# Expert products in the batches of blocks 0 to 2: a half-cost floor on the planner's PE budget

## The chip, the cores and the metric

The kernel runs on one core of one Trainium2 chip. The metric is device time in microseconds (us), the median over executions: 1169.55 us before the change (three runs, 1169.44 to 1170.32). The profile is of one further execution. Its engines are called PE (the matrix engine), DVE (vector), ACT (scalar), POOL and SP, as in the profile.

## The reference, cut to what matters

Two transformer layers over x, four sequences of 512 tokens, 256 wide, all in float32. The change touches the plan of layer 0 only.

```python
x = x + attn0(layernorm(x))      # 16 heads of 16, causal, softmax
x = x + experts(layernorm(x))    # below
x = x + attn1(layernorm(x))      # 16 heads of 128, 4 kv heads; mixes the 4 sequences at one position
x = x + mlp(layernorm(x))        # gelu(gate) * up, 2048 wide, 4-bit weights

# experts: 8 of them, one choice of two for every token AND output column
logits = (h @ router_w.T + router_b).reshape(T, 256, 8)
w, sel = top_k(softmax(logits), 2);  w = w / w.sum()
c      = zeros(T, 8).at[t, sel].add(w)          # summed over the 256 columns
final  = einsum('te,teo->to', c, h @ expert_w.T + expert_b)
```

For each group of 128 tokens the experts need two sets of 256x2048 products, one for the router's logits and one for the experts' outputs, and between them a long elementwise search for the two greatest of eight logits.

## The kernel before, in words

**Layer 0's attention** runs in 44 batches. Block j holds 512 rows: a quarter of the positions of all four sequences. A batch is one block, one sequence s and some of the four groups of four heads: all four groups in block 0 (batches 0 to 3), two in block 1 (4 to 11), one in blocks 2 and 3 (12 to 27 and 28 to 43). The loop at L833 does the following for batch n, and every engine but SP runs its instructions in exactly this order:

- `greatest(n+1)`, L652: PE computes the scores of the next batch, into four of the five PSUM tiles of `ps_sc` (L454).
- `shift(n)`: PE transposes the maxima (`mxT`, L681), DVE subtracts them from the queries (`qk`, L684).
- `mask(n+1)`: PE adds the causal mask (L665), DVE takes the maxima, four reductions (L671), which lets those PSUM tiles go.
- **slot a**: a call of `fill` (L849).
- `mixed(n-1)`, L736: PE multiplies the previous batch's probabilities with the values.
- `powers(n)`: PE computes the shifted scores (L700) into four tiles of `ps_sc`, ACT takes exp of each (L709), which lets them go.
- **slot b**: a call of `fill` (L857).

**fill** is a planner that works while the program is written out: it fixes the order, and nothing of it runs on the chip. It gives PE and DVE a budget in about microseconds (PE 2.0 and 2.4 in slots a and b of blocks 0 and 1, 1.8 and 2.2 in block 2, 1.6 and 2.0 in block 3; DVE 2.6 in each). What was overdrawn in the slot before is taken off; what was left over is lost. It then goes through the streams in their order, and takes a stream's next piece as long as that engine's budget is above zero and the piece's own condition holds. A piece may overdraw.

The streams that matter here, in the order in which they are asked:

- `divided` (L748): the end of a sequence's attention: `av_T`, `oq_T`, and after a block's last sequence two output products of cost 1.75 (L783).
- `hidden_pieces` (L264): the second layernorm of a finished block and its transposes.
- `addition_pieces` (L341): DVE adds the experts' weighted outputs (L350 to L352), cost 1.55 for half a group.
- `total_pieces` and `weight_pieces` (L432, L355): DVE's search over one group's logits, 17 steps in all. It starts with L371 and L373, cost 1.25 each, and ends with eight steps of 0.95 (L423, L426). Group g's search starts only in a slot after the one that wrote its last logit product. `weights[g]` is set when a group is done.
- `result_pieces` (L302): the expert products `eo`, cost 1.85, four to a group; ACT scales and evicts each (L323).
- `logit_pieces` (L282): the logit products `lg_ps`, cost 1.85, four to a group; ACT copies each out (L297).

Both kinds of product wait on `made()`, the number of the search's steps planned so far divided by 17. With the group under search counted as k, its steps release products in this order: eo 0 of group k-1 at step 0, lg 0 of group k+1 at 2, then eo 1 at 4, lg 1 at 6, eo 2 at 8, lg 2 at 10, eo 3 at 12 and lg 3 at 13. All products are `dense` (L228): two fp32 matmuls, which the profile shows as four rows of 128x512.

What is not done at the end of layer 0's attention is worked off in layer 1's attention. There `between` (L1124) gives a `fill` after nearly every piece, with a PE budget of `1.9 * share + 0.2`; `share` (L1141) is the number of products still open over the slots up to step 8, and is zero from step 9. At step 10 a loop (L1128) plans whatever is then left.

Of the kernel before, what the change touches and what calls it, by code (L numbers as in the profile page):

```python
# [32 lines left out]
def tile_transformer(  # L33
# [75 lines left out]

    slot = 0

    def need(engine, cost, gap=0, cond=None):
        return engine, cost, gap, cond
# [1 line left out]
    class Stream:  # L117
# [4 lines left out]
        def ready(self, left):  # L122
            if self.next is None:
                return False
            engine, cost, gap, cond = self.next
            return left[engine] > 0 and slot >= self.last + gap and (cond is None or cond())

        def go(self):
            engine, cost = self.next[:2]
# [17 lines left out]
    left = {"PE": 0.0, "DVE": 0.0}  # L147
# [113 lines left out]
    logits, weights, halves = {}, {}, {}  # L261
# [187 lines left out]
    with ExitStack() as l0:  # L449
# [377 lines left out]
        done = blanked = 0  # L827
# [479 lines left out]
```

## Time and profile before

| What | Value |
|---|---|
| Median of three runs | 1169.55 us |
| Profiled execution, its own time | 1170.3 us |
| Its span on the core | 1168.6 us |
| Granted PE clock, mean | 1.00 |
| Logit products, L234 `lg_ps` | 122.5 us busy, 256 rows |
| Expert products, L234 `eo` | 121.5 us busy, 256 rows |
| DVE's maxima, L671 | 100.4 us busy, 176 rows |
| PE idle while DVE waits: `qk` L684 for `mxT` | 29.0 us in 14 waits |

The span covers all but 1.7 us of the profiled execution. The busy time of PE counts rows whose ends are modelled and which overlap, and a matmul that is held up by a wait shows as a long row; so PE's 98% does not say that it never waits. Time stamps below are us from the start of the span. Layer 0's attention runs from about 26 to 376 us, layer 1's attention from about 394 to 834, and the mlp to the end. Batches 12 to 27, block 2, lie between about 127 and 250 us.

### The profile page before, as it was taken

How to read it: one execution, taken by the hardware profiler on the slowest of the kernel's cores; microseconds unless marked ns; L12 is line 12 of the kernel's file. 1: busy time of each engine (PE TensorE's matmuls, PEld its weight loads, DVE VectorE, ACT ScalarE, POOL GpSimd, SP SyncE). 2: the span in 40 equal slices, each digit the busy share in tenths (PEclk: the TensorE clock that was granted, in tenths of full speed). 3: DMA queues.
4: the chain of work that ended last, by engine and by line, in shares of the span. 5: the costliest groups of instructions: out<-in, count | busy, mean ns of one | idle time of the engine just before them, and what ended most of it. 6: DMA issues, size and time to landing. Idle time of an engine off the chain costs nothing.

```text
span 1168.6 us, 18563 instructions
## 1 busy us (share of the span) xinstructions
PE 1142.0 (98%) x7178; PEld 661.5 (57%) x7178; DVE 809.8 (69%) x1783; ACT 484.3 (41%) x1099; POOL 108.4 (9%) x152
## 2 busy tenths in 40 slices
PE   7999999999999999999999999999999999999998
PEld 3666555556554445555555555566644475484487
DVE  5676889999988953868773785687699845716710
ACT  1444645556555542444443444544344312303300
POOL 7322221212112000000000000000000000000000
PEclk9999999999999999999999999999999999999999
DMA  7230110000000500000000001120110000000000
GB/s 219 64 83 2 19 20 2 2 1 2 2 2 1 181 1 1 1 1 1 1 1 1 1 1 46 28 54 21 27 46 1 0 1 19 0 1 19 1 18 19
DMA packets 21239, 26.46 MB, mean 23 GB/s; under 512 B 5128, under 2 KB 14600, under 8 KB 21152
## 3 DMA queue, kind: packets, MB, share of 16 engines
q1 hardware_dynamic: 20480, 24.10, 7.5%
q10 hardware_dynamic: 672, 1.18, 0.4%
q8 instruction: 56, 0.92, 0.3%
q14 instruction: 31, 0.25, 0.1%
HBM read 18.97 MB, written 2.10 MB: 18 GB/s over the span
## 4 chain that ended last, share of the span: by engine, by line
PE 81%; DVE 13%; ACT 2%; issue 1%; POOL 1%; DMA 0%; SPq 0%; ACTq 0%; DVEq 0%; POOLq 0%
PE qk_ps L987 11%; PE y L1234 9%; PE o L1078 9%; PE g L916 9%; PE u L916 9%; PE lg_ps L234 8%; PE eo L234 7%; PE s L652 3%; PE s L700 3%; DVE mx L671 3%; PE av L736 2%; PE v_ps L969 2%; PE qk_ps L545 2%; PE a L1058 1%; PE s L1000 1%
## 5 line engine op out<-in xcount | busy, mean ns | idle before, releaser
L987 PE MATMUL qk_ps<-xT,wqkv 128*128 128x512 f32 x320 | 148.9, 599 | 2.3 <-ACT part L323 1.2
L234 PE MATMUL lg_ps<-rw,xT 128*128 128x512 f32 x256 | 122.5, 601 | 1.4 <-ACT xT L954 0.3
L234 PE MATMUL eo<-ew,xT 128*128 128x512 f32 x256 | 121.5, 600 | 0.8 <-ACT lg L297 0.5
L1078 PE MATMUL o<-wpj,oT 128*128 128x256 f32 x512 | 119.1, 382 | 0.0
L1234 PE MATMUL y<-wd,it 128*128 128x256 f32 x512 | 111.8, 379 | 0.0
L1078 PEld LDWEIGHTS o<-wpj,oT 128*128 128x128 f32 x512 | 95.9, 190 | 27.5 <-issue 14.3
L1234 PEld LDWEIGHTS y<-wd,it 128*128 128x128 f32 x512 | 97.0, 190 | 15.0 <-issue 2.2
L671 DVE TENSOR_REDUCE mx<-s 128x1 f32<-128x384 f32 (+3 forms) x176 | 100.4, 632 | 1.3 <-PE s L665 1.3
L987 PEld LDWEIGHTS qk_ps<-xT,wqkv 128*128 128x128 f32 x320 | 59.1, 190 | 71.4 <-issue 57.4
L709 ACT ACTIVATE pt<-s 128x512 f32<-128x512 f32 (+1 forms) x176 | 84.1, 563 | 35.3 <-PE s L700 35.3
L916 PE MATMUL g<-xT,wgu 128*128 128x512 f32 x192 | 90.4, 593 | 0.0
L916 PE MATMUL u<-xT,wgu 128*128 128x512 f32 x192 | 90.2, 592 | 0.0
L323 ACT ACTIVATE part<-eo,c 128x256 f32<-128x256 f32 x128 | 53.7, 472 | 85.2 <-PE eo L234 75.2
L719 POOL TENSOR_SCALAR_AFFINE_SELECT pt<-pt 128x256 f32<-128x256 f32 (+2 forms) x88 | 63.2, 725 | 249.8 <-ACT pt L709 249.3
L1212 ACT ACTIVATE th<-sq 128x512 f32<-128x512 f32 x64 | 40.3, 630 | 87.6 <-DVE sq L1211 87.6
L234 PEld LDWEIGHTS lg_ps<-rw,xT 128*128 128x128 f32 x256 | 46.1, 190 | 46.1 <-issue 37.3
L234 PEld LDWEIGHTS eo<-ew,xT 128*128 128x128 f32 x256 | 46.1, 190 | 45.7 <-issue 38.3
L222 DVE TENSOR_TENSOR xres<-xres,y 128x256 f32<-128x256 f32 x16 | 6.7, 421 | 92.5 <-PE y L1234 92.5
L185 POOL TENSOR_TENSOR ln_rs<-rs_v,minus_half 128x4 f32<-128x4 f32 x16 | 17.6, 1099 | 552.2 <-DVE rs_v L184 439.9
L297 ACT COPY lg<-lg_ps 128x512 f32<-128x512 f32 x64 | 37.6, 588 | 73.5 <-PE lg_ps L234 73.5
L1213 DVE SCALAR_TENSOR_TENSOR th<-th,g 128x512 f32<-128x512 f32 x63 | 43.2, 686 | 29.2 <-ACT th L1212 29.2
L916 PEld LDWEIGHTS u<-xT,wgu 128*128 128x128 f32 x192 | 36.5, 190 | 45.9 <-issue 44.7
(233 smaller groups left out, 1776.8 us busy)
## 6 DMA issues: line engine op xcount, KB each, us to landing
qk<-stage SPq DMA_DIRECT2D x56, 64.0 KB, 2.4
wqkv<-in_w_qkv SPq DMA_DIRECT2D x8, 320.0 KB, 6.8
rw<-in_router_w SPq DMA_DIRECT2D x8, 256.0 KB, 7.8
ew<-in_expert_w SPq DMA_DIRECT2D x8, 256.0 KB, 4.6
wpj<-in_w_proj SPq DMA_DIRECT2D x1, 2048.0 KB
out<-xres SPq DMA_DIRECT2D x4, 512.0 KB, 2.6
xres<-in_x SPq DMA_DIRECT2D x3, 512.0 KB, 9.0
dq_wgu<-in_gate_w SPq DMA_DIRECT2D x8, 128.0 KB, 2.4
```

The source lines that it names most:

```text
L234: nc.tensor.matmul(ps, lhsT=xT[:, hc, (g % 4) * P : (g % 4 + 1) * P], rhs=w[:, hc, 2 * pair : 2 * pair + 2, :].rearrange("p e o -> p (e o) ...
L297: nc.scalar.copy(lg[:, 2 * pair : 2 * pair + 2, :].rearrange("p e o -> p (e o)"), ps)
L323: nc.scalar.mul(part[:, e % 4], ps[:, i], c[:, e : e + 1])
L671: nc.vector.tensor_reduce(maxes[n % 2][:, h, gs[0] : gs[0] + nb], ps[:, : nb * nk].rearrange("p (b k) -> p b k", b=nb), AX.X, ALU.max,)
L709: nc.scalar.activation(pt[:, i, : nb * nk], tiles[2 * pair + i][:, : nb * nk], AF.Exp, scale=0.25)
L719: nc.gpsimd.affine_select(out=last, in_=last, compare_op=ALU.is_ge, fill=0.0, base=0, pattern=pattern, channel_multiplier=-1,)
L916: nc.tensor.matmul(ps, lhsT=wgu[:, w, half, jj, par * P : (par + 1) * P], rhs=xT[:, half, :], start=half == 0, stop=half == 1,)
L987: nc.tensor.matmul(ps, lhsT=wqkv[:, hc, kv, h, :], rhs=xT[:, hc, :], start=hc == 0, stop=hc == 1,)
L1078: nc.tensor.matmul(ys[t // 2][:, t % 2], lhsT=state["o"][:, h, t * P : (t + 1) * P], rhs=wpj[:, HPK * kv + h, :], start=kv == 0 and h == 0 ...
L1212: nc.scalar.activation(th, sq, AF.Tanh, scale=0.7978845608028654)
L1213: nc.vector.scalar_tensor_tensor(th, th, 1.0, gp, ALU.add, ALU.mult)
L1234: nc.tensor.matmul(ps, lhsT=it[:, c // 2, c % 2, t * P : (t + 1) * P], rhs=wd[:, c // 2, c % 2, :], start=c == 0, stop=c == 2 * NJ - 1,)
```

## The change: a product is planned only while half its cost is left

```diff
-    slot = 0
+    slot = done = 0
...
             engine, cost, gap, cond = self.next
-            return left[engine] > 0 and slot >= self.last + gap and (cond is None or cond())
+
+            least = cost / 2 if engine == "PE" and cost > 1.8 and weights and done < 28 else 0.0
+            return left[engine] > least and slot >= self.last + gap and (cond is None or cond())
```

Only the two kinds of product have a PE cost above 1.8. For them the budget must now exceed 0.925 and not just zero. `weights` is empty until the search over group 0 is done, so the rule begins there. `done` counts the batches whose powers are planned; it is 28 after `powers(27)`, so the last slot under the rule is slot a of batch 27. The loop's own `done = blanked = 0` (L827) now sets the name that line 112 has introduced. No instruction is added, removed or changed in kind.

## The prediction

> **What bounds the kernel.** I read the page first (engines, chain), then the busy time by stages, then the chain of waits and the timelines of PE and DVE between 150 and 255 us, the only stretch in which the rule acts, and last the waits of the later stages. The stages (PE, PEld, DVE, ACT, POOL busy, then the granted clock):
>
> ```profile
> 154.00:250.00 96.00, 94.59 (x949) 50.83 (x945) 89.19 (x219) 55.33 (x157) 20.92 (x27) 1.00 0.01 1
> 440.00:706.00 266.00, 264.02 (x1258) 148.34 (x1257) 177.56 (x440) 115.36 (x302) 1.01 (x1) 1.00 0.00 1
> ```
>
> In layer 1 (second row) PE is full and DVE has a third of its time free. Work that the change pushes from layer 0 into layer 1 therefore costs there what it saves before. In block 2 (first row) PE and DVE are both above 92%, and hand over to each other in every batch: `shift` on DVE needs `mxT` from PE, `powers` on PE needs `shift` and the reductions. What one engine loses by the other's late handover is the only thing that a new order can win. The chain from batch 22 to 24 shows such a loss:
>
> ```profile
> 211.95 1.91 PE eo L234 x4
> 213.86 1.72 PE lg_ps L234 x4
> 215.58 0.86 PE s L652 x8
> 216.44 0.26 PE mxT L681
> 216.70 0.22 PE s L665 x4
> 216.92 1.77 PE lg_ps L234 x4
> 218.69 0.79 PE av L736 x24
> 219.49 0.88 PE s L700 x24
> 220.37 2.29 PE s L652 x6
> 222.66 0.26 PE mxT L681
> ```
>
> Slot b of batch 22 holds a pair, eo and lg; slot a of 23 one lg; slot b of 23 nothing, for the powers (L700) are followed at once by the next scores (L652). These take 2.29 us where the same work took 0.86 five lines above: the trace shows their weights waiting for ACT's exps, which must empty the PSUM tiles. While the pair ran, DVE had used its share and stood:
>
> ```profile
> 216.74 0.29 DVE L684 TENSOR_TENSOR qk<-qk,mxT 128x128 f32<-128x128 f32 x1 [2.09 <-PE mxT L681]
> 246.05 0.29 DVE L684 TENSOR_TENSOR qk<-qk,mxT 128x128 f32<-128x128 f32 x1 [1.62 <-PE mxT L681]
> ```
>
> The second line is the same pattern one group later (pair in slot b of batch 26, nothing in slot b of 27, where the scores take 2.68 against 1.14 us). A third, weaker pair stands in slot b of batch 17: DVE waits 1.05 us at 180.79, and both slots of batch 19 are empty (`powers` 1.42 against 0.95, scores about 2.5 against 0.93).
>
> **The change part by part.** *What it forbids.* After one product of 1.85 at most 2.4 - 1.85 = 0.55 is left, under 0.925, so no slot under the rule takes two. After an output product (1.75) at most 0.65 is left: none there either. A debt of more than about 0.9 also shuts a slot of 1.8, but with one product per slot debts stay near 0.2. From 154 to 248 us, 25 slots hold 23 products. The demand fits one to a slot; three pairs must be split, and one product that now stands beside an output product's debt (lg at 151.5, slot a of 14) is put off.
>
> *Its price on PE.* In the chain a product behind another takes 1.72 us, behind the mask 1.77, behind the powers 1.91. Some six products change place: at most 6 x 0.19 = 1.1 us, mostly 0.05 each; I take 0.3, and it is inside the steps below. [...] The row has clock 1.00 throughout 154 to 250 us, though the stalls are in it; the gaps now get shorter. I take the row: nothing.
>
> *First product, 151 us.* Put off to slot a of 16, which pushes the next lg to the empty slot b there. From 151 to 173 us DVE is busy without a break (L684 at 159.63 stands behind five search steps), so the earlier end on PE is worth nothing, and the later extra 1.9 us lies where PE waits for DVE anyway (`oq`, `xn` at 172). Nothing either way; without that cover it would be 1.9 us moved.
>
> *Pair of batch 17.* Without the second product the scores of batch 18 end about 1.5 us earlier, and DVE's `shift` 1.04 us earlier: it ends its own work at 179.75. The three products behind it move one place; the last fills slot a of 19. Followed forward, batch 20's powers, held up by 0.41 us (`av`) and 0.58 us (`powers` 1.53 against 0.95), come **1.4 us** earlier.
>
> *Pair of batch 22.* DVE goes from 214.65 straight into `shift`: about 2 us more for it. PE has lg 2 in slot a of 23 and lg 3 in slot b; that fills the hole before the scores. The 1.43 us of stall (2.29 - 0.86) goes, less 0.3 for the product's later start: PE is **1.1 us** further ahead, 2.5 in all. What is late next: lg 3 now comes in slot b of 23, so the next search cannot start there. L371 and L373 (2.5 of budget) slip one slot and DVE's gain goes into idle time.
>
> *Pair of batch 26.* By the step counts, eo 2 (step 8) is not yet released in slot a of 26, because the search is late and step 8 must wait one slot more. It goes to slot b, eo 3 to slot a of 27, and lg 2 and lg 3 come together in slot b of 27, where the rule has ended. A hole (26a) and a pair (27b) remain, in place of a pair (26b) and a hole (27b); the shift of 27 still comes without DVE's wait of 1.62 us, about half of which reaches PE: **0.8 us**. Sum 1.4 + 1.1 + 0.8 = 3.3 us at 250 us, with as many products done as before, but the search one slot behind (two steps of 0.95 and L371: 3.15 of budget).
>
> *Block 3, given back.* In slot a of 28 lg 0 now lacks its step and slips to slot b. The empty slot costs about what the reductions outlast the mask and `av`: 2.48 (L671) + 0.3 - 0.8 - 0.9 = 1.1 us at most, nothing if the product fills a later hole (slot b of 36, where the scores take 2.12 against 1.14). I take 0.6. Block 3's small budgets then keep its slots at one product each, one product behind; that one ends up in layer 1 at cost. No DMA, POOL or SP instruction moves past another one; `sum_up` on ACT keeps its place relative to its steps.
>
> Sum: 3.3 - 0.6 = **2.7 us less**: 1170.3 - 2.7 = 1167.6 for the profiled execution, and with the 0.75 us by which that lies above the median, 1166.8 us.
>
> **The rivals.** *Moved, not removed* (1168.5; within 0.2%, which is 2.3 us and about what a measurement of this kernel can tell). For it: half of what I count at each pair is DVE time that DVE then idles away, and in block 3 both engines are again above 92% with a pipeline in a worse phase, so 28a, 30 and 41 may each cost 0.5 to 1 us. Against: the scores' long rows are PE's own loss, and PE's time decides the end.
>
> *Holes elsewhere, too* (1163.5): a smoother train also closes holes in block 3 (DVE waits 2.51 at 328.93 and 1.65 at 361.24, `o0` waits 1.74 for `aT` at 382.12). Against: the rule is off there.
>
> *The search starves* (1174). Every group's lg 3 comes at step 13 and lies at the end of a row of four products released within six steps. At one to a slot it is a slot late, and DVE loses up to 2.6 of budget for each group. If this does not stop after two groups but carries through block 3, where slots have less PE budget, four to six groups lose a slot each and PE gets holes of about 1.1 us each: 4 to 6 us, or 1174. It decides if by the end of layer 0 two or more further products are open. In layer 1 the last search step of group 15 is at 691.3 us and step 8's last slot at about 703; if the search is over 12 us late there, the last products fall where `share` is zero and wait for one another, some 3 us more. For it: period and slots agree to the digit (8 slots and 8 products to a group), so no slot is spare for a late one. Against: DVE waits 5.01 and 2.33 us in layer 1's tail, so there the search is waited for by nobody but itself.
>
> *The rule hardly acts*: it decides only where the budget lies between 0 and 0.925; 3 pairs and one single product here. That is in the sums.
>
> **How the numbers follow.** Forecast 0.45 (1165.0 to 1168.2), holes elsewhere 0.07, moved but not removed 0.25, starved 0.23. Forecast and holes give faster 0.52. For 8 in 10: from 1163.0, below the hole case, to 1172.0, within the starved one; 4 to 6 us above is cut off.
>
> **What would show it.** Right: no two products side by side between 154 and 248 us; no scores row above 2 us at about 220; DVE's waits of 2.09 and 1.62 us gone; the first 32x512 scores (244.61 before) some 3 to 5 us earlier; the first layer-1 product (394.51) about 4 us earlier, with one product less before it. Wrong: if that mark comes earlier only by the 1.72 us of each product left out, nothing was won; if L371 of groups 3 to 7 comes later than at 221.34, 252.29, 294.45 and 331.81, the search is starved[...].

## The result, and the profile after

| Kernel | Median | Runs |
|---|---|---|
| before | 1170.26 us | 6 |
| after | 1175.39 us (1173.14 to 1176.82) | 6 |

The ratio is 1.0046, with a 95% interval of [1.0036, 1.0056]: the change makes the kernel slower by 5.1 us, where 2.7 us less was forecast, and the time lies above the range (1163.0 to 1172.0). The profiled execution of after is its fastest run, 1173.14 us, with a span of 1171.4. In the code after the change every line behind the edit stands two further down: L236 is the products, L673 the maxima, L686 `qk`.

First the busy time by stages, after; columns as before (length, then PE, PEld, DVE, ACT, POOL busy, the granted clock, the DMA's share and GB/s).

```profile
154.00:250.00 96.00, 93.47 (x956) 49.38 (x960) 90.68 (x225) 57.28 (x162) 18.56 (x29) 1.00 0.01 1
250.00:376.00 126.00, 121.06 (x1385) 68.51 (x1374) 110.76 (x262) 71.16 (x183) 22.30 (x34) 1.00 0.01 2
```

The same stretch of block 3, before, which the prediction did not print:

```profile
250.00:376.00 126.00, 123.10 (x1405) 68.59 (x1404) 116.10 (x264) 73.30 (x192) 22.29 (x35) 1.00 0.01 2
```

In block 2, where the rule acts, DVE now does more in 96 us (90.68 against 89.19). In block 3, where the rule is off, DVE does 5.3 us less and PE 2.0 us less. That is the first sign that the loss is not where the edit is.

**Block 2 gives the sum that was forecast.** The chain of waits of after, at the batches that the prediction showed (start, length, engine, tile, line, rows):

```profile
209.68 1.91 PE eo L236 x4
211.59 0.86 PE s L654 x8
...
212.93 1.77 PE lg_ps L236 x4
...
216.38 1.91 PE lg_ps L236 x4
218.29 0.86 PE s L654 x8
```

The pair is gone: one product in slot b of 22, one in slot a and one in slot b of 23, and the scores that took 2.29 us take 0.86. DVE's waits of 2.09 and 1.62 us, which were to go, have not gone; each stands one batch later. From DVE's timeline (start, length, and in brackets the idle time before it):

```profile
219.45 0.29 DVE L686 TENSOR_TENSOR qk<-qk,mxT 128x128 f32<-128x128 f32 x1 [2.01 <-PE mxT L683]
249.18 0.29 DVE L686 TENSOR_TENSOR qk<-qk,mxT 128x128 f32<-128x128 f32 x1 [1.79 <-PE mxT L683]
```

Added up over 154 to 250 us, DVE waits 3.8 us for `mxT`, against 5.3 before.

**Marks, compared.** Every batch has one `mxT`, and by it the two traces can be laid side by side. Differences to before in us, with the shift of the whole trace at batch 0 taken off; "open" is how many products fewer had been done by then, and the last column adds 1.75 us for each of them (the length of a product behind another or behind the mask):

| Mark | Before | After | open | at equal work |
|---|---|---|---|---|
| `mxT` of batch 20 | 192.20 | -0.4 | 0 | -0.4 |
| batch 22 | 207.95 | -2.2 | 0 | -2.2 |
| batch 24 | 222.59 | -3.4 | 0 | -3.4 |
| batch 28 | 252.12 | -3.2 | 0 | -3.2 |
| batch 29 | 260.01 | -4.9 | 2 | -1.4 |
| batch 37 | 321.04 | -5.1 | 2 | -1.6 |
| batch 40 | 343.35 | -3.1 | 3 | +2.1 |
| batch 43 | 366.29 | -3.2 | 2 | +0.3 |
| first layer-1 product | 394.51 | -2.7 | 3 | +2.5 |
| scores of step 1 of layer 1 | 446.24 | -0.6 | 4 | +4.6 |
| scores of step 9 | 690.11 | +2.9 | 0 | +2.9 |

(Step 1 has one `v_ps` product more done, which is taken off.) Up to batch 28 the change wins 3.2 us, almost to the digit what was forecast. Then it loses in four places (and wins 1.8 us back between batches 40 and 43).

*Batch 28* loses 1.8 us. DVE's timeline of after, the end of one search and the start of the next:

```profile
252.45 0.42 DVE L425 SCALAR_TENSOR_TENSOR junk<-lg,w 128x256 bf16<-128x256 f32 x1
252.80 1.22 DVE L373 TENSOR_TENSOR hi<-lg 128x1024 f32<-128x1024 f32 x1
...
254.22 0.42 DVE L764 TENSOR_TENSOR oq<-av_T,rden 128x256 f32<-128x256 f32 x1
254.56 1.22 DVE L375 TENSOR_TENSOR lo<-lg 128x1024 f32<-128x1024 f32 x1
```

Slot a of 28 holds the last two steps of the old search and only the first of the new; the second comes behind `oq`, in slot b; the third, which releases lg 0, in slot a of 29. So neither slot of 28 has a product. On PE:

```profile
250.31 2.16 PE L702 MATMUL s<-qk 32*128 32x128 f32 x32
...
252.98 2.12 PE L654 MATMUL s<-qk 32*128 32x512 f32 x8
```

The powers take 2.16 and the scores 2.12 us; with products around them, in the third experiment below, they take 1.23 and 1.14. A stall does not stand as a gap here. It stands as a long row.

*Batches 37 to 39* lose 3.7 us. Before, each of them has one product in slot a and one in slot b and takes 7.35 to 7.53 us. After, slot a is empty in all three, and slot b has a pair in the first two. Batch 37, from PE's timeline:

```profile
317.66 1.08 PE L738 MATMUL av<-pt,va 128*32 128x128 f32 x32 [0.99 <-DVE qk L686]
318.67 1.94 PE L702 MATMUL s<-qk 32*128 32x128 f32 x32
320.54 1.98 PE L236 MATMUL eo<-ew,xT 128*128 128x512 f32 x4
322.36 1.88 PE L236 MATMUL lg_ps<-rw,xT 128*128 128x512 f32 x4
```

The same batch before, from PE's timeline:

```profile
321.66 1.88 PE L234 MATMUL lg_ps<-rw,xT 128*128 128x512 f32 x4
323.47 1.08 PE L736 MATMUL av<-pt,va 128*32 128x128 f32 x32
324.48 1.17 PE L700 MATMUL s<-qk 32*128 32x128 f32 x32
325.58 1.98 PE L234 MATMUL lg_ps<-rw,xT 128*128 128x512 f32 x4
```

Batch 37 takes 9.35 us against 7.53 for the same two products: the 0.99 us of waiting and the 0.77 us that the powers are longer are nearly all of the difference. The edit took pairs out of block 2, and they came back in block 3.

*The start of layer 1*, 2.2 us. Before, `v_ps` follows the transposes `xT_ps` without a wait. Now ACT has six sums of `sum_up` ahead of the copies of `xT`, and PE waits for them:

```profile
391.72 7.13 PE L971 MATMUL v_ps<-wqkv,xT 128*128 128x512 f32 x16 [2.20 <-ACT xT L956]
```

*Step 0 of layer 1*, 2.6 us between the scores of steps 0 and 1 at equal work (one product less and one `v_ps` more stand between them; 0.5 us are won ahead of them), with these transposes late:

```profile
420.25 1.65 PE L212 MATMUL xT_ps<-ident,xn 128*128 128x128 f32 x8 [1.30 <-DVE xn L196]
434.73 1.71 PE L212 MATMUL xT_ps<-ident,xn 128*128 128x128 f32 x8 [0.73 <-ACT th L392]
```

From there to step 9, 1.7 us are won back, and the rest of the kernel keeps its distance to the end. From batch 28 to the end this trace loses 6.1 us (from -3.2 to +2.9). The 2.2 us from this run (1173.14) to the median (1175.39) are not in it at all; the first experiment is about them.

**Theory.** The rule wins what was forecast, and puts the search behind in doing so; the late search is what costs, through the slots that have nothing released, and the holes cost a second time by the clock behind them (1.5 and 1.6 us in the profiles of experiments 1 and 8). **Rivals**: the loss comes from the split of the products itself; from the sums on ACT at the start of layer 1; or from the clock alone.

### The profile page after: what moved, and what is told of

Read it like the earlier page. It is cut to its first block, busy times and chain, and to the rows that moved or that the text cites. A ratio compares the mean times of both kernels' runs of the same rounds, so it can differ in the third digit from the quotient of the medians.

```text
span 1171.4 us, 18555 instructions
## 1 busy us (share of the span) xinstructions
PE 1140.1 (97%) x7178; PEld 661.2 (56%) x7178; DVE 807.7 (69%) x1783; ACT 485.5 (41%) x1099; POOL 104.6 (9%) x152
## 4 chain that ended last, share of the span: by engine, by line
PE 81%; DVE 14%; ACT 2%; issue 1%; POOL 1%; DMA 1%; SPq 0%; DVEq 0%; ACTq 0%; POOLq 0%
PE qk_ps L989 11%; PE y L1236 9%; PE o L1080 9%; PE g L918 9%; PE u L918 9%; PE lg_ps L236 8%; PE eo L236 7%; PE s L702 3%; PE s L654 3%; DVE mx L673 3%; PE v_ps L971 2%; PE av L738 2%; PE qk_ps L547 2%; PE s L1002 1%; PE a L1060 1%
## 5 line engine op out<-in xcount | busy, mean ns | idle before, releaser
L236 PE MATMUL lg_ps<-rw,xT 128*128 128x512 f32 x256 | 122.2, 600 | 2.3 <-ACT part L325 0.9
L236 PE MATMUL eo<-ew,xT 128*128 128x512 f32 x256 | 121.0, 598 | 0.5 <-ACT lg L299 0.5
L673 DVE TENSOR_REDUCE mx<-s 128x1 f32<-128x384 f32 (+3 forms) x176 | 100.5, 633 | 1.2 <-PE s L667 1.2
L721 POOL TENSOR_SCALAR_AFFINE_SELECT pt<-pt 128x256 f32<-128x256 f32 (+2 forms) x88 | 59.9, 685 | 244.5 <-ACT pt L711 244.2
L236 PEld LDWEIGHTS lg_ps<-rw,xT 128*128 128x128 f32 x256 | 46.0, 190 | 47.1 <-issue 38.0
L236 PEld LDWEIGHTS eo<-ew,xT 128*128 128x128 f32 x256 | 46.6, 190 | 44.6 <-issue 39.0
```

What stands on the lines that cost most here:

```text
L236: nc.tensor.matmul(ps, lhsT=xT[:, hc, (g % 4) * P : (g % 4 + 1) * P], rhs=w[:, hc, 2 * pair : 2 * pair + 2, :].rearrange("p e o -> p (e o) ...
L673: nc.vector.tensor_reduce(maxes[n % 2][:, h, gs[0] : gs[0] + nb], ps[:, : nb * nk].rearrange("p (b k) -> p b k", b=nb), AX.X, ALU.max,)
L721: nc.gpsimd.affine_select(out=last, in_=last, compare_op=ALU.is_ge, fill=0.0, base=0, pattern=pattern, channel_multiplier=-1,)
```

## The experiments

**1. After, once more**, unchanged, to see where its time varies.

> The changed kernel once more, for a profile of a run in which the granted clock is below 1.00. Theory 'clock': the hole of PE before the first products of layer 1 (389.5 to 391.7 us in the first profile, behind six sums on ACT) is what lets the clock fall, so the rows below 1.00 begin within 5 us behind it, and the time lies 2 to 3.5 us above 1173. Rival 'elsewhere': the clock falls at another place, such as block 3's empty slots or the start of the kernel, and then also in runs of the kernel before. Time 1173 to 1177.

Measured: 1175.26 us (1172.88 to 1176.67, four runs), ratio 1.0044 [1.0030, 1.0058]. The run with mean clock 1.00 took 1172.88, those below it 1175.08 to 1176.67. The profiled one took 1175.08; its busy time in steps of 1 us at the start of layer 1 (the clock is the third number from the end):

```profile
390.00:391.00 1.00, 0.00 (x0) 0.00 (x0) 0.97 (x3) 1.00 (x6) 0.00 (x0) 1.00 1.01 374
391.00:392.00 1.00, 0.00 (x0) 0.00 (x0) 0.97 (x5) 1.00 (x6) 0.00 (x0) 0.91 1.01 358
392.00:393.00 1.00, 0.91 (x1) 0.50 (x2) 1.00 (x5) 0.52 (x2) 0.00 (x0) 0.50 1.04 394
```

PE is idle for two microseconds (the wait for the copies of `xT`), and then runs at half clock (0.50 in the rows from 392 to 395, 0.89 in the next) to 395.2 us. From its timeline:

```profile
392.09 8.67 PE L971 MATMUL v_ps<-wqkv,xT 128*128 128x512 f32 x16 [2.19 <-ACT xT L956]
```

The same 16 rows took 7.13 us in the other profile of this program. These 1.5 us are most of the 1.9 us by which this run is longer (1175.08 against 1173.14); the other 0.4 us lie ahead of batch 0. So the hole costs its length, 2.2 us, and in this run 1.5 us more. The other runs below 1.00 have no profile, so the place in them is not shown. A mean clock below 1.00 is no proof by itself: experiment 2's runs at 0.999 (1166.93, 1166.98 and 1167.44 us) are among its fastest, and so are before's at 0.998 (1168.88 to 1169.23 us).

**2. The rule up to batch 21 only**: the pair of batch 17 is split and the product of slot a of 14 put off, as in after; the pairs of 22 and 26 stay.

```diff
-            least = cost / 2 if engine == "PE" and cost > 1.8 and weights and done < 28 else 0.0
+            least = cost / 2 if engine == "PE" and cost > 1.8 and weights and done < 22 else 0.0
```

> The rule ends at batch 21, so only the pair of batch 17 is split and every later slot and the search stand as before. Theory 'search': no group's search starts later, so the 1.5 us won by batch 21 stay to the end: 1168.7, and the clock stays at 1.00. Rival 'given back': what is won in layer 0 is lost again at the end of layer 0 whatever the search does: 1170.2 or more.

Measured: 1167.79 us (18 runs), ratio 0.9982 [0.9974, 0.9989]. By the marks it is 2.2 us ahead at batch 22 and 2.3 at the end, with the same number of products done at each mark from there on. The split itself wins, more than the 1.5 us expected, and the win lasts to the end when the search's starts stay in their slots.

**3. The rule as in after, with the search on time.** The output products eo 3 of groups 1 and 2 are held back until the powers of 24 and of 28 batches are planned. So lg 2 and lg 3 of groups 3 and 4 take the slots, and the searches of these groups start in the same batches as before. Beside it `total_pieces` is asked ahead of `addition_pieces`.

```diff
+    held = {(1, 3): 24, (2, 3): 28}
...
-                    and (made() >= h + 1 + 0.22 * pair or not logits),
+                    and (made() >= h + 1 + 0.22 * pair or not logits)
+                    and done >= held.get((h, pair), 0),
...
-            inputs[1], fold, Stream(addition_pieces()), Stream(counted(total_pieces())),
+            inputs[1], fold, Stream(counted(total_pieces())), Stream(addition_pieces()),
```

> All three pairs are split, but the logit product keeps its slot and the expert product (group 1 product 3, group 2 product 3) is the one that moves to the empty slot; the total of a group is asked before the additions, so that every group's search starts in the same batch as before the change. Theory 'search': the 3.3 us won by batch 28 stay: 1166 to 1167.5, clock 1.00, 65 products done before layer 1 as in the kernel before. Rival 'given back': 1169.5 to 1175, as the gain is lost in block 3 and behind it whatever the search does.

Measured: 1165.51 us (1164.97 to 1166.25), ratio 0.9963 [0.9951, 0.9976]: faster than both kernels, by 4.6 us against before. By the marks it is 4.8 us ahead at batch 28 and 4.6 at the end. Its stages:

```profile
154.00:250.00 96.00, 94.97 (x976) 49.69 (x977) 93.91 (x228) 57.82 (x165) 20.25 (x29) 1.00 0.01 2
250.00:376.00 126.00, 120.27 (x1370) 66.25 (x1362) 115.42 (x270) 71.52 (x184) 23.83 (x34) 1.00 0.01 2
```

DVE does 93.91 us in block 2 and has 115.42 left in block 3, where after had 110.76. And its search starts, from DVE's timeline:

```profile
215.10 1.23 DVE L375 TENSOR_TENSOR hi<-lg 128x1024 f32<-128x1024 f32 x1
244.82 1.42 DVE L375 TENSOR_TENSOR hi<-lg 128x1024 f32<-128x1024 f32 x1
288.11 1.23 DVE L375 TENSOR_TENSOR hi<-lg 128x1024 f32<-128x1024 f32 x1
326.46 1.22 DVE L375 TENSOR_TENSOR hi<-lg 128x1024 f32<-128x1024 f32 x1
```

The same four starts stand at 221.34, 252.29, 294.45 and 331.81 before, and at 221.79, 252.80, 305.41 and 338.36 after. The rule is the same in this kernel and in after; the slots of the search are not.

**4. After, with ACT's copies first.** In one slot at the start of layer 1 the search's sums are emitted behind the copies for which `v_ps` waits.

```diff
-    def fill(**budget):
+    def fill(late=False, **budget):
...
-        emit_deferred(False)
+        if not late:
+            emit_deferred(False)
...
+        emit_deferred(False)
         emit_deferred(True)
...
+        at = slot + 2
         while inputs.next is not None:
-            fill(PE=2.0, DVE=3.0)
+            fill(slot + 1 == at, PE=2.0, DVE=3.0)
```

> The changed kernel, but in the slot that transposes layer 1's first input the sums of the search are given to ACT behind the two copies and not ahead of them. Theory 'ACT queue and clock': PE's wait of 2.2 us before layer 1's first products falls to about 0.4, and with it the clock stays at 1.00 in all runs: 1170.5 to 1171.5. Rival 'the wait moves': the search is a slot later instead, layer 1 waits for it, and the time stays at 1173 to 1175; rival 'clock from elsewhere': the profile's 2 us go but the runs still spread with clocks of 0.996 to 0.999, 1172 to 1175.

Measured: 1172.27 us (1171.61 to 1173.91, 15 runs), ratio 1.0022 [1.0014, 1.0029]. PE's timeline at the place:

```profile
390.45 5.85 PE L973 MATMUL v_ps<-wqkv,xT 128*128 128x512 f32 x13 [1.01 <-ACT xT L958]
```

The wait shrinks from 2.20 to 1.01 us and the end of the trace comes 1.3 us earlier (against 1173.14, the profiled run of after); but the median falls by 3 us. The theory's numbers are missed: the wait did not fall to 0.4, and nine of the 15 runs have a clock of 0.998 or 0.999, so the rival 'clock from elsewhere' holds in part. The other 1.7 us of the median fit the clock, but are not shown to be it: behind the shortened hole it is not lowered in either of the two runs of this kernel that were profiled (the other is experiment 8).

**5. The late search alone**: the kernel before, with no rule, and group 3's search held back by one slot. From batch 28 on its order of products is that of after.

```diff
+    late = {3: 1}
...
-            yield need("DVE", 1.25, cond=lambda: g in logits and logits[g][1] < slot)
+            yield need("DVE", 1.25, cond=lambda: g in logits and logits[g][1] + late.get(g, 0) < slot)
```

> The kernel before, without the rule; only the search of group 3 starts one slot later than its logits would allow. The plan behind batch 27 is then product for product that of the changed kernel, while the three pairs of products stay. Theory 'search': this alone brings the loss: some 6 us (what the changed kernel lost between batch 28 and the end in its first profile, -3.3 to +2.8), so 1175 to 1177, and above it where the clock falls behind the same hole at the end of layer 0, up to 1179. Rival 'the split itself': the loss belongs to the products that no longer run back to back, and a late search costs nothing that layer 1 doesn't hide: 1169.5 to 1171.5.

Measured: 1178.94 us (1176.38 to 1180.52, five runs), ratio 1.0073 [1.0060, 1.0085]. Two runs at mean clock 1.00 took 1176.38 and 1176.50, that is 6.4 and 6.5 us more than before's 1169.96. By the marks the profiled run (mean clock 0.996) loses in the same places as after: 1.8 us at batch 28, 3.7 from batch 37 to 40, 2.2 from batch 43 to the first layer-1 product, and 3.7 from there to step 1 (after: 2.1), with half clock from 395.8 to 399.2. It also loses 1.8 us between batches 24 and 28, where the low clock shown below lies. One slot of delay of one search, with no split, is enough for the whole loss: 6.4 us here, where after loses 6.1 behind batch 28. This trace also has half clock behind a wait of PE for `qk` (1.33 us, to 237.3):

```profile
239.00:240.00 1.00, 1.00 (x18) 0.95 (x14) 1.00 (x2) 0.07 (x1) 0.00 (x0) 0.50 0.00 0
```

And it has a third such stretch, from 191.0 to 194.4 us, where its plan is still that of before. There one product takes 3.17 us and not 1.94, but nothing is lost in the end: DVE is busy for 0.93 to 1.00 of each row of 1 us, the mark of batch 21 comes 0.6 us late, and at batch 22 the mark stands where it stood. Half clock on PE cost nothing by then.

**6. The rule through all of layer 0**: it holds to batch 43, so block 3 has no pairs either.

```diff
-            least = cost / 2 if engine == "PE" and cost > 1.8 and weights and done < 28 else 0.0
+            least = cost / 2 if engine == "PE" and cost > 1.8 and weights and done < 44 else 0.0
```

> The rule through block 3 too (to batch 43 and not 27). Theory 'search': slots of block 3 have less budget, lg 3 of a group comes later still, and layer 0 leaves as many products or more to layer 1: 1174 to 1178. Rival 'holes elsewhere': the pairs in slots 37b and 38b of the changed kernel and the empty slots beside them go, and block 3 gives back what it lost: 1167 to 1171.

Measured: 1171.75 us (1170.12 to 1174.83, 20 runs), ratio 1.0016 [1.0009, 1.0023]. It lies between the two ranges and in neither, and below the theory's. The searches start as late as in after or later (batches 24, 28, 36, 40, 43 for groups 3 to 7), one product more is open at the end of layer 0, and yet eight runs at clock 1.00 took 1170.12 to 1171.10, hardly more than before. With the 3.2 us won up to batch 28, about 3.6 us are lost behind it, where after loses 6.1. So a late search costs here too, but how late it is does not set how much. The slots that its products get seem to matter: where they come one to a slot, batches 37 to 40 lose 1.95 us at equal work, where after loses 3.7. The rest of the difference is not traced.

**7. The second edit of the third experiment alone**, in the kernel before: the order of the two streams of sums.

> The kernel before with one edit: the stream that forms Block 3's sums is asked for work ahead of the stream of additions, the other half of the edit of e3_search_on_time. TensorE's order stays that of before; 12 instructions of VectorE in layer 1 change places. Theory (what won in e3_search_on_time was the search of groups 3 and 4 at its old place with the pairs' products put off): 1169.5 to 1170.5, the same as before. Rival 'streams' (the order of the sums is what won): 1166 to 1168.

Measured: 1169.83 us (12 runs), ratio 0.9999 [0.9990, 1.0007]. The order of the streams alone does nothing, so what won in the third experiment needs the first edit, by which the products are put off and the search is not. Whether the second edit adds something to the first was not run.

**8. The kernel of experiment 4 once more**, for the place where its clock falls.

> The kernel of e4_copies_first once more, for the place where its clock falls. Theory (holes cost by the clock that follows them): in a run whose mean clock is under 1.00 there are 3 to 4 us at clock 0.50 right behind a stretch in which TensorE is idle for over 1 us, most likely the one at 233 to 235 us, and the time is 1172.7 to 1173.9; in a run at 1.00 there is no such place and the time is 1171.6 to 1172.1. Rival 'elsewhere': the low clock stands at a place where TensorE was busy throughout.

Measured: 1173.01 us, mean clock 0.999. Of all stretches of 10 us only the one from 230 to 240 has a clock below 1.00. From its PE timeline:

```profile
234.45 0.86 PE L740 MATMUL av<-pt,va 128*32 128x128 f32 x24 [1.32 <-DVE qk L688]
...
236.94 3.39 PE L238 MATMUL eo<-ew,xT 128*128 128x512 f32 x4
```

And its busy time in steps of 1 us:

```profile
236.00:237.00 1.00, 1.00 (x19) 0.78 (x19) 1.00 (x2) 0.30 (x1) 0.00 (x0) 0.70 0.00 0
237.00:238.00 1.00, 1.00 (x3) 0.48 (x3) 0.96 (x4) 1.00 (x4) 0.30 (x1) 0.50 0.00 0
```

This is the hole that the empty slot a of batch 26 makes. Two microseconds after it, at 236.4 us, the clock is halved, a product that took 1.98 us in experiment 4 takes 3.39, and by the marks of batches 26 and 28 this run loses 1.6 us against the profiled run of experiment 4. That is nearly all that parts the two runs (1173.01 against 1171.87, with 0.4 us of the 1.6 given back ahead of batch 0).

## Why the prediction was wrong, by its own steps

- **First product, 151 us: nothing,** and **pair of batch 17: 1.4 us.** Right in kind, and only seen as a sum: the mark of batch 17 comes 1.2 us later at equal work, that of batch 22 comes 2.2 us earlier. Experiment 2, which has these two steps alone, confirms 2.3 us.
- **Pair of batch 22: 1.1 us.** Right in size: 1.2 us between batches 22 and 24. DVE's wait of 2.09 us went there, and as the step said, its gain went into idle time: it waits 2.01 us one batch later. The late start of the next search, named there, came too.
- **Pair of batch 26: 0.8 us.** It gave 0.2 us away instead. The step named the hole in slot a of 26 and put no price on it (PE waits 1.3 us there for `qk`), and DVE's wait did not go but moved one batch on (1.79 us). With the search on time the same stretch wins 1.4 us in experiment 3.
- **Sum at 250 us: 3.3 us, with as many products done and the search one slot behind.** Right on all three counts, the first with some luck, as 17 gave more and 26 less than its term: 3.2 us, 32 products, and the two end steps with L373 behind them in slot a of 28.
- **Block 3, given back: 0.6 us.** This is the step that failed. It let lg 0 slip to slot b of 28 and then kept "one product each, one product behind". The step that releases lg 0 did not fit into slot b, because `rden` and `oq` take DVE's budget there, a charge that the prediction does not mention; both slots of 28 stayed empty, for 1.8 us. And the delay did not stay at one product: the search of group 5 starts two batches later than before (305.41 against 294.45), three products are open at the end of layer 0, and the slots have the empty-a, pair-in-b pattern that the change was to remove. What was put at 0.6 us is 6.1 us in the trace of after, at clock 1.00, and experiment 5 makes 6.4 us out of the late search alone. Experiment 3, with the search on time, loses 0.3 us there.
- **The clock, taken at 1.00 and put at nothing.** Wrong as well, as to the whole kernel. The row with clock 1.00 is true of before; it says nothing of holes that the change makes. In the traces, six of the seven stretches of half clock found where PE had work stand behind such holes (the seventh, at 191 us in experiment 5, has only long rows ahead of it): it cost 1.5 us behind the one at 390 (experiment 1) and 1.6 us behind the one at 233 (experiment 8), and in both cases another profile of the same program has the hole and not the half clock. Why the clock fell in one run and not in the other is not shown. In experiment 8 the product that was caught is one of a split pair (slot b of 26), and it took 1.4 us more (3.39 against 1.98). The median of after lies 2.4 us above its two runs at clock 1.00 (1172.88 and 1173.14); that the clock makes all of this is argued from one profile.

The sum: 3.2 us won up to batch 28, 6.1 us lost behind it, which the late search brings (experiments 3 and 5), and 2.2 us from the profiled run to the median, which fit the clock: 5.1 us slower, as measured. Of the rivals it is **the search starves**, at 1174 us with 0.23, that came; its point of decision, two or more further products open at the end of layer 0, was met with three. That its own price, a slot per group at 1.1 us each, had about the right size is in part luck: it was not DVE's lost budget in each group, but PE's waits at four places and the clock.

Not settled: why the stretch between the scores of steps 0 and 1 of layer 1 loses 2.6 us (the waits for `xn` and for `th` are seen, the order that causes them was not undone on its own), why experiment 6 loses less with a search as late, and why the hole in slot a of 26 halved the clock in the traces of three kernels (experiments 5, 6 and 8) but not in the profile of after with clock 1.00, nor in that of experiment 4.

## What to carry to other kernels

In a plan where one engine's products feed another engine's long search and the search releases the next products, ask of each reordering first whether the search still starts in its slot; a slot lost there came back later as empty slots and pairs, and cost more than the reordering won. Put off what only waits to be added (here eo 3) rather than what the search waits for (lg 2, lg 3). And when a plan makes a new idle stretch on PE, count it for its length, and leave room in the range for the clock behind it (1.5 us in experiment 1, 1.6 in experiment 8).

## What the runs showed of the hardware

Behind a wait of PE of 1.3 us in slot a of batch 26 (1.32 to 1.34; from 233.1 to 234.5 us in experiment 8) the clock was halved in three of the five profiles that show this wait (experiments 5, 6 and 8; not in after, nor in experiment 4), and behind one of 2.2 us (2.19 to 2.27) at the start of layer 1 in three of four (experiments 1, 5 and 6; not in after). The low clock lasted about 3.4 us in five of these cases and the one at 191 us: summed from the rows in steps of 1 us, 0.6 + 1 + 1 + 0.8 us in experiment 8, and 0.2 + 3 + 0.2 in experiment 1. In experiment 6, behind the wait of 2.27 us, it lasted about twice that: the rows of 10 us have 0.97 from 380 and 0.68 from 390, which is about 0.6 + 6.4 us at 0.50, and `v_ps` took 10.21 us and not 7.13.

The length of a wait alone does not decide: the profiles of before (382.12 us) and of experiment 3 (376.76) both have a wait of 1.74 us, with clock 1.00 in the rows around it, and ahead of the low clock at 191 us in experiment 5 the last wait of PE that stands as a gap is one of 0.16 us, at 186.8 (its scores there, from 188.7, stand as long rows, up to 191.3). A wide spread of a kernel's runs (3.7 us for after, 4.1 and 4.7 for experiments 5 and 6, against 1.9 for before and 1.3 for experiment 3) went with the holes at slot a of 26 and at the start of layer 1.
